# Conv taps in halves and TensorE's side work spread over the sixteen steps of a block

## The chip, the cores and the metric

The kernel runs on one core of a Trainium2 chip. The metric is the device time of one execution in microseconds (us). One execution is also recorded by the hardware profiler; durations and waits come from that one.

## The reference

Input x has shape (8, 128, 128, 128), fp32, in the order batch, channel, row, column. Two layers follow each other, and all arithmetic stays in fp32.

```python
# layer 0: dilated conv to 64 channels, batch norm, gelu, 2-D FFT, channel attention and a gate, inverse FFTs, + x
x = layer0(x)
# layer 1
y   = conv3x3(x, conv_w) + conv_b                    # 128 -> 128 channels
seq = y.reshape(B * H * W, 8, 16)                    # 8 tokens of 16 channels from each row of 128 numbers
out = mamba(seq)                                     # d_inner 32, d_state 16, 8 sequential steps:
      # h = dA * h + dBx ;  y_t = sum over d_state of h * C ;  then gate by silu(z), project back to 16
xp  = silu(group_norm(out.reshape(B, C, H, W), 4 groups) * gn_w + gn_b)
return x + xp
```

The reshape is a plain one: an image row of one channel, 128 columns long, is one sequence of 8 tokens. The state of a sequence has 32 x 16 numbers.

## The kernel before

Layer 0 handles two images at a time: a convolution phase, an attention phase and a spectrum phase. It ends at about 2.95 ms in the trace; the change leaves it alone.

Layer 1 (`layer1`) cuts the eight images into 256 blocks of RB = 4 rows, each 128 channels x 512 positions. After the transposition in `turn` the 128 partitions hold what belongs to one sequence, and N = 512 sequences lie along the free dimension. The 8 tokens are the time steps t of the recurrence; each is worked in two halves, so a block has NS = 16 steps s, with t = s // 2. The order on each engine is written out by hand: `step(i, s)` issues, for block i and its neighbours, what belongs to step s, and under the manual schedule every engine keeps that order.

What step s of block i issues, in this order:

- At s = 0, `lay_out(i, 1)` (SP's queue): 8 DMAs that spread dt and u over partitions (`du`, 64 KB each) and 8 that copy B and C to all places (`bb`, `cc`, 256 KB each, read from the tile `bc1`). Then `load(i + 2)`: at every second block a load of ten rows of the layer's input (`xin`, 640 KB).
- `spreads` of the next step: TensorE makes `da` (L543, only if t > 0) and `ups` (L544), two matmuls each on 16 rows of the array. An fp32 matmul appears as two passes in the profile. ScalarE turns `da` into an exponential (L546).
- At s = 15 `project_x(i + 2)`, at s = 0 `project_dt(i + 1)`, at s = 1 and 2 `project_bc(i + 1, 0)` and `(i + 1, 1)`, whose results ScalarE copies from PSUM to the tiles `bc0` and `bc1` (L515).
- `project_out(i - 1)` (L602) in the steps of the table OUT, `conv(i + 2)` (L134) in those of the table CONV (nine taps, each a matmul of up to 512 columns), and `turn(i + 2)` (L476) at one step. The `halves` behind the three projections of the item before are L484, `project_bc` is L513.
- `advance`: VectorE multiplies `da` by the state of the step two before and adds `h` (L567, L568). In the steps of ON_POOL the addition goes to GpSimd, and VectorE does one operation instead of two (L564, then L565 on GpSimd).
- `inject` of the next step: VectorE makes the new `h` from `ups` and `bb` (L553). `inject` j is the one that starts the state of step j.
- At s = 1 `inputs(i + 1)` on VectorE; `weigh` on GpSimd (h times `cc`, L574); at s = 15 `project_z(i + 2)`.
- Four steps behind, `collect` (TensorE, L583, every second step) sums over d_state, and at two places, s = 3 and s = 11, `skip` (TensorE, L589) and `gated` (VectorE, L594, tile `ym`) end half a block's sum.
- At s = 8 `lay_out(i + 1, 0)` and the loads of the last stage; at s = 3 the last addition on GpSimd and the store of a result block. `keep` (bn_stats on VectorE, then a store of the block for the group norm) and, at an image's end, `norm_of`.

The tiles that matter: PSUM holds `ups` once, `da` twice, `yps` once and `pm` once. Everything that isn't `ups`, `da` or `yps` uses `pm` by turns, through `misc()`:

```python
p_m = ctx.enter_context(tc.tile_pool(name="l1_pm", bufs=1, space=PSUM))
def misc():
    return p_m.tile([P, RB, W], F32, name="pm")
```

`bc0`, `bc1`, `y` and `yT` have one buffer each (pool wk1), `du`, `bb` and `cc` two, the states `h` five and the products `hc` six.

Of the kernel before, what the change touches and what calls it, by code (L numbers as in the profile page):

```python
# [9 lines left out]
F32 = mybir.dt.float32  # L10
# [6 lines left out]
P = 128  # L17
C = 128
H = 128
# [97 lines left out]
def _taps(dil):  # L117

    t = [(ky, kx) for ky in range(3) for kx in range(3)]
    t.remove((1, 1))  # L120
    return [(ky * 3 + kx, (ky - 1) * dil, (kx - 1) * dil) for ky, kx in [(1, 1)] + t]


def _conv_taps(nc, outs, wt, srcs, base, r, dil, k0=0, k1=9):

    taps = _taps(dil)
    for n in range(k0, k1):
        t, dy, dx = taps[n]  # L130
        a, b = max(0, -(r + dy)), min(4, H - (r + dy))
        wa, wb = max(0, -dx), min(W, W - dx)
        for out, src in zip(outs, srcs):
            nc.tensor.matmul(  # L134
                out[:, a:b, wa:wb], wt[:, t, :],
                src[:, r + dy + a - base:r + dy + b - base, wa + dx:wb + dx],
                start=(n == 0), stop=(n == len(taps) - 1),
            )


# [203 lines left out]
def layer1(ctx, tc, x1, w1, c1, out):  # L344
# [8 lines left out]
    nc = tc.nc  # L353
# [5 lines left out]
    wt = const.tile([P, W1_N], F32, name="l1_wt")  # L359
# [3 lines left out]
    def cf(name):  # L363
        at, n = C1[name]
        return ct[:, at:at + n]

    def wf(name):
        at, n = W1[name]
        return wt[:, at:at + n]

    convw = wf("conv_w").rearrange("p (t c) -> p t c", c=C)
# [15 lines left out]
    taps = cf("taps").rearrange("p (k l) -> p k l", l=L)  # L387
    w_k = wf("conv1d_w").rearrange("p (k d) -> p k d", d=DI)
    with tc.tile_pool(name="l1_prep", bufs=2) as prep:
# [19 lines left out]
        for hf in range(NH):  # L409
            for l in range(L):  # L410
                k = hf * L + l
# [14 lines left out]
    RB = 4  # L426
    N = RB * C
    GP = 2
    NS = L * NG // GP
    wk1 = ctx.enter_context(tc.tile_pool(name="l1_w1", bufs=1))  # L430
    wk2 = ctx.enter_context(tc.tile_pool(name="l1_w2", bufs=2))
# [8 lines left out]
    blocks = [(b, r) for b in range(B) for r in range(0, H, RB)]  # L440
    nb = len(blocks)
    st8 = [{} for _ in blocks]
    xins, stats, gns, tails = {}, {}, {}, []
    ON_POOL = (5, 8, 11, 14)

    def live(i):
        return 0 <= i < nb

    def misc():
        return p_m.tile([P, RB, W], F32, name="pm")  # L450

    def load(i):
        b, r = blocks[i]
        if r % CH == 0:
            lo, hi = max(0, r - 1), min(H, r + CH + 1)
            xin = wk2.tile([P, CH + 2, W], F32, name="xin")
            nc.sync.dma_start(xin[:, :hi - lo, :], x1[b][:, lo:hi, :])
            xins[b, r // CH] = xin, lo
        st8[i]["xin"] = xins[b, r // CH]

    def conv(i, k0, k1):
        d = st8[i]
        if k0 == 0:
            d["pm"] = misc()
        xin, lo = d["xin"]
        _conv_taps(nc, [d["pm"]], convw, [xin], lo, blocks[i][1], 1, k0, k1)
        if k1 == 9:
            y = wk1.tile([P, RB, W], F32, name="y")
            nc.scalar.activation(y, d["pm"], AF.Identity, bias=wf("conv_b"))
            d["y"] = y  # L470
# [16 lines left out]
    def project_x(i):  # L487
        d = st8[i]
        ps = halves([m_xh[:, hf, :] for hf in range(NH)], [d["yT"]] * NH)
        d["xc"] = wk3.tile([P, NH, N], F32, name="xc")  # L490
        nc.scalar.activation(d["xc"], ps, AF.Silu, bias=wf("conv1d_b"))
# [13 lines left out]
    def inputs(i):  # L505
        d = st8[i]
        d["u"] = wk2.tile([P, NH, N], F32, name="u")
        nc.vector.tensor_mul(d["u"], d["dt"], d["xc"])
# [8 lines left out]
    def lay_out(i, hf):  # L517

        d = st8[i]
        du = wk2.tile([P, LP, N], F32, name="du")  # L520
        bb = wk2.tile([P, LP, N], F32, name="bb")
        cc = wk2.tile([P, LP, N], F32, name="cc")
        for q in range(NG):
            for k, v, g in ((0, d["dt"], q), (8, d["u"], (q + GP) % NG)):
                nc.sync.dma_start(du[q * DI + k:q * DI + k + 8], v[g * DI:(g + 1) * DI, hf, :])
        for lp in range(LP):
            for k, v in ((0, bb), (1, cc)):
                at = (k * LP + lp) * DS
                nc.sync.dma_start(
                    v[:, lp, :], d["bc", hf][at:at + DS, :].unsqueeze(1).broadcast_to([DS, 8, N]))  # L530
        d["du", hf], d["bb", hf], d["cc", hf] = du, bb, cc
# [24 lines left out]
    def advance(i, s):  # L556
# [3 lines left out]
        if t:  # L560
            da, before = d["da", s], d["h", s - 2]
            if s in ON_POOL:
                ah = wk1.tile([P, GP, N], F32, name="ah")
# [26 lines left out]

    def gated(i, hf):
        d = st8[i]
        d["ym", hf] = wk1.tile([P, N], F32, name=f"ym{hf}")
        nc.vector.tensor_mul(d["ym", hf], d["yps"], d["zs"][:, hf, :])  # L594

    def project_out(i, k0, k1):
# [12 lines left out]
    def keep(i):  # L609
        d, (b, r) = st8[i], blocks[i]  # L610
        if r == 0:
            gns[b] = dram.tile([C, H, W], F32, name="gn")
            stats[b] = wk2.tile([P, H // RB, nc.vector.BN_STATS_DIM], F32, name="st")
        nc.vector.bn_stats(stats[b][:, r // RB, :], d["xr"].rearrange("p a b -> p (a b)"))
        nc.sync.dma_start(gns[b][:, r:r + RB, :], d["xr"])
        d.clear()

    def norm_of(b):

        mv = wk2.tile([P, 2], F32, name="mv")  # L620
        gmv = wk2.tile([P, 2], F32, name="gmv")
        dv = wk2.tile([P, 1], F32, name="dv")
        sc = wk2.tile([P, 1], F32, name="sc")
        bi = wk2.tile([P, 1], F32, name="bi")
        nc.vector.bn_aggr(mv, stats[b])
        ps = misc().rearrange("p a b -> p (a b)")
        nc.tensor.matmul(ps[:, 0:2], cf("group"), mv, start=True, stop=True)
        nc.vector.tensor_copy(gmv, ps[:, 0:2])
        nc.vector.tensor_sub(dv, mv[:, 0:1], gmv[:, 0:1])
        nc.vector.tensor_mul(dv, dv, dv)  # L630
        ps = misc().rearrange("p a b -> p (a b)")
        nc.tensor.matmul(ps[:, 0:1], cf("group"), dv, start=True, stop=True)
        nc.vector.tensor_scalar(sc, ps[:, 0:1], gmv[:, 1:2], GN_EPS, ALU.add, ALU.add)
        nc.scalar.activation(sc, sc, AF.Sqrt)
        nc.vector.reciprocal(sc, sc)
        nc.vector.tensor_mul(sc, sc, wf("gn_w"))
        nc.vector.tensor_mul(bi, gmv[:, 0:1], sc)
        nc.vector.tensor_sub(bi, wf("gn_b"), bi)
        tails.extend((b, r, sc, bi) for r in range(0, H, RB))
# [11 lines left out]
    def last_act():  # L651
        b, r, sc, bi, v, res = fin["active"] = fin.pop("loaded")
        nc.scalar.activation(v, v, AF.Silu, bias=bi, scale=sc)  # L653
# [3 lines left out]
        nc.gpsimd.tensor_add(res, res, v)  # L657
        nc.sync.dma_start(out[b, :, r:r + RB, :], res)  # L658

    CONV = {7: (0, 2), 8: (2, 3), 9: (3, 5), 10: (5, 6), 11: (6, 7), 12: (7, 8), 13: (8, 9)}  # L660
    OUT = {5: (0, 5), 6: (5, 8)}

    def step(i, s):

        ni, ns = (i, s + 1) if s + 1 < NS else (i + 1, 0)
        if s == 0:
            if live(i):
                lay_out(i, 1)  # L670
            if live(i + 2):
                load(i + 2)
        if live(ni):
            spreads(ni, ns)
        if s == 15 and live(i + 2):
            project_x(i + 2)
        if s == 0 and "loaded" in fin:
            last_act()
        if s == 0 and live(i + 1):
            project_dt(i + 1)  # L680
        if s in (1, 2) and live(i + 1):
            project_bc(i + 1, s - 1)
        if s in OUT and live(i - 1):
            project_out(i - 1, *OUT[s])
        if s in CONV and live(i + 2):
            conv(i + 2, *CONV[s])
        if s == 14 and live(i + 2):
            turn(i + 2)
        if live(i):
            advance(i, s)  # L690
        if live(ni):
            inject(ni, ns)
        if s == 1 and live(i + 1):
            inputs(i + 1)
        if live(i):
            weigh(i, s)
        if s == 15 and live(i + 2):
            project_z(i + 2)

        gi, gs = (i, s - 4) if s >= 4 else (i - 1, s - 4 + NS)  # L700
        if live(gi):
            if gs % 2 == 0:
                collect(gi, gs // 2)
            if gs in (7, 15):
                skip(gi, gs // 8)
                gated(gi, gs // 8)
        if s == 8:
            if live(i + 1):
                lay_out(i + 1, 0)
            if tails:  # L710
                last_load()
        if s == 3 and "active" in fin:
            last_sum()
        if s == 7 and live(i - 1):
            keep(i - 1)
        if s == 3 and live(i - 2) and blocks[i - 2][1] + RB == H:
            norm_of(blocks[i - 2][0])

    E = mybir.EngineType
    with tc.manual_schedule(engines={E.PE, E.Activation, E.DVE, E.Pool, E.SP}):  # L720
# [92 lines left out]
```

## Time and profile before

| | |
|---|---|
| median of 3 runs | 19169.76 us (19157.88 to 19195.24) |
| the profiled execution, its own time | 19192.02 us |
| its span in the profile | 19190.2 us |
| mean granted TensorE clock | 0.862 |
| TensorE matmul busy | 18443.3 us (96%) |
| VectorE busy | 13878.4 us (72%) |
| GpSimd busy | 12632.6 us (66%) |
| ScalarE busy | 7032.3 us (37%) |
| DMA engines, mean busy share | 45.9% on SP's queue |

A matmul's end is modelled in the profile, and TensorE counts as busy while a matmul runs at half clock, so the 96% is no measure of how much of the array is used. The granted clock is listed for any stretch of time. Of a group of instructions the profile gives the busy time and mean duration, then the idle time of its engine just before them and the instruction that ended most of it. In a list of stretches each line has the stretch, its length, the busy time of TensorE (matmuls), TensorE's weight loads, VectorE, ScalarE and GpSimd with their counts of instructions, then the granted clock, the DMA engines' busy share and GB/s. In a timeline a line has the start, the duration, the engine (SPq: a DMA issue on SP's queue), the line of the kernel and the operation; brackets tell how long the engine was idle before it.

### The profile page before, as it was taken

What the parts mean: (1) busy time and instruction counts of PE and PEld (TensorE: products, weight loads), DVE (VectorE), ACT (ScalarE), POOL (GpSimd) and SP (SyncE); (2) the same over time, 40 slices, a digit from 0 to 9 for tenths busy, and PEclk for the clock granted to TensorE, in tenths of its full rate; (3) what the DMA queues carried; (4) which work ended last, traced back from release to release, by engine and by line L of the source; (5) the groups of instructions that cost most, each with busy time, mean ns of one, the idle gap of its engine ahead of it and who ended that gap; (6) DMA issues with size and microseconds to landing.
All of it is one profiled execution on the core that took longest, in us unless ns stands there. A gap on an engine that the chain in (4) does not pass through costs nothing. (4 is left out here: it accounts for less than half of the span.)

```text
span 19190.2 us, 208781 instructions
## 1 busy us (share of the span) xinstructions
PE 18443.3 (96%) x74920; PEld 6645.5 (35%) x74920; DVE 13878.4 (72%) x14203; ACT 7032.3 (37%) x7703; POOL 12632.6 (66%) x5636
## 2 busy tenths in 40 slices
PE   8998999999999999999999999999999999999997
PEld 3554553333333333333333333333333333333332
DVE  1441447778778877787788877887787878877885
ACT  1131223333333433333334333433333333333333
POOL 0010015777777777777777777777777777777776
PEclk9999998888888888888888888888888888888886
DMA  2222224444455555555555545555555555555555
GB/s 85 70 76 83 75 73 91 93 96 94 97 106 106 107 105 106 108 104 104 108 106 106 109 102 107 108 108 104 106 107 106 106 105 108 105 104 109 106 106 122
DMA packets 1075786, 1932.99 MB, mean 101 GB/s; under 512 B 123968, under 2 KB 255040, under 8 KB 1058368
## 3 DMA queue, kind: packets, MB, share of 16 engines
q1 hardware_dynamic: 1001472, 1850.17, 45.9%
q10 hardware_dynamic: 73280, 69.47, 1.3%
q8 instruction: 596, 9.76, 0.2%
q14 instruction: 438, 3.59, 0.1%
HBM read 375.64 MB, written 201.33 MB: 30 GB/s over the span
## 5 line engine op out<-in xcount | busy, mean ns | idle before, releaser
L574 POOL TENSOR_TENSOR hc<-h,cc 128x1024 f32<-128x1024 f32 x4096 | 9604.0, 2356 | 3447.5 <-PE pm L513 1304.7
L553 DVE TENSOR_TENSOR h<-ups,bb 128x1024 f32<-128x1024 f32 x4096 | 4993.9, 1219 | 2903.9 <-PE ups L544 2546.7
L543 PE MATMUL da<-du,m_a 16*128 16x512 f32 x14336 | 6343.9, 728 | 210.0 <-DVE h L568 193.2
L546 ACT ACTIVATE da<-da 128x1024 f32<-128x1024 f32 x3584 | 3617.9, 1010 | 7110.2 <-PE ups L544 7106.1
L544 PE MATMUL ups<-du,m_u 16*128 16x512 f32 x16384 | 5410.2, 737 | 9.7 <-DVE h L553 2.6
L568 DVE TENSOR_TENSOR h<-da,h 128x1024 f32<-128x1024 f32 x2560 | 3134.0, 1224 | 87.8
L567 DVE TENSOR_TENSOR da<-da,h 128x1024 f32<-128x1024 f32 x2560 | 3132.2, 1224 | 65.0 <-ACT da L546 62.8
L543 PEld LDWEIGHTS da<-du,m_a 16*128 16x128 f32 x14336 | 1789.2, 206 | 3402.2 <-DVE h L568 1717.1
L583 PE MATMUL yps<-hc,l_ct 128*32 128x512 f32 x16384 | 2824.9, 769 | 1.7 <-POOL hc L574 1.7
L565 POOL TENSOR_TENSOR h<-ah,h 128x1024 f32<-128x1024 f32 x1024 | 2420.7, 2364 | 392.0 <-DVE ah L564 391.8
L134 PE MATMUL pm<-xin,l_wt 128*128 128x508 f32 (+1 forms) x4608 | 2447.4, 632 | 5.2 <-DMA l_wt<-w 4.6
L544 PEld LDWEIGHTS ups<-du,m_u 16*128 16x128 f32 x16384 | 1410.6, 207 | 1661.3 <-DVE h L553 1015.8
L134 PEld LDWEIGHTS pm<-xin,l_wt 128*128 128x128 f32 x4608 | 732.8, 189 | 1616.3 <-issue 1613.0
L272 POOL TENSOR_TENSOR xr<-xr,sq 128x512 f32<-128x512 f32 x128 | 160.5, 1266 | 1652.6 <-ACT sq L271 1603.5
L564 DVE TENSOR_TENSOR ah<-da,h 128x1024 f32<-128x1024 f32 x1024 | 1240.9, 1212 | 0.0
L602 PEld LDWEIGHTS pm<-m_o,ym 128*128 128x128 f32 x4096 | 909.7, 327 | 767.1 <-issue 766.3
L134 PE MATMUL cps<-xin,l_wt 128*64 128x500 f32 (+2 forms) x4608 | 1026.7, 584 | 39.1 <-issue 30.2
L602 PE MATMUL pm<-m_o,ym 128*128 128x128 f32 x4096 | 1060.1, 440 | 0.6 <-DVE ym L594 0.6
L222 DVE COPY fT<-tps 128x512 f32<-128x512 f32 x128 | 88.5, 692 | 1182.2 <-PE tps L221 1182.2
L583 PEld LDWEIGHTS yps<-hc,l_ct 128*32 128x32 f32 x16384 | 355.4, 119 | 1354.9 <-issue 1282.3
L338 POOL TENSOR_TENSOR og<-og,xg 128x512 f32<-128x512 f32 x128 | 164.4, 1285 | 967.1 <-ACT og L337 831.6
L515 ACT COPY bc<-pm 128x512 f32<-128x512 f32 x512 | 301.6, 589 | 1041.0 <-DMA cc<-bc 594.9
(145 smaller groups left out, 13471.5 us busy)
## 6 DMA issues: line engine op xcount, KB each, us to landing
bb<-bc SPq DMA_DIRECT2D x2048, 256.0 KB
cc<-bc SPq DMA_DIRECT2D x2048, 256.0 KB
du<-dt SPq DMA_DIRECT2D x2048, 64.0 KB
du<-u SPq DMA_DIRECT2D x2048, 64.0 KB
xin<-x SPq DMA_DIRECT2D x112, 640.0 KB
xin<-x SPq DMA_DIRECT2D x48, 1408.0 KB
gn<-xr SPq DMA_DIRECT2D x256, 256.0 KB
v<-gn SPq DMA_DIRECT2D x256, 256.0 KB
```

The lines of the kernel that those rows point to most:

```text
L134: nc.tensor.matmul(out[:, a:b, wa:wb], wt[:, t, :], src[:, r + dy + a - base:r + dy + b - base, wa + dx:wb + dx], start=(n == 0), stop=(n ...
L543: nc.tensor.matmul(da[:, q], m_a[a:a + 16, :], du[a:a + 16, lp, :], start=True, stop=True)
L544: nc.tensor.matmul(ups[:, q], m_u[u:u + 16, :], du[u:u + 16, lp, :], start=True, stop=True)
L546: nc.scalar.activation(da, da, AF.Exp)
L553: nc.vector.tensor_mul(h, d["ups", s], bb[:, lp:lp + 1, :].broadcast_to([P, GP, N]))
L564: nc.vector.tensor_mul(ah, da, before)
L565: nc.gpsimd.tensor_add(h, ah, h)
L567: nc.vector.tensor_mul(da, da, before)
L568: nc.vector.tensor_add(h, da, h)
L574: nc.gpsimd.tensor_mul(hc, d["h", s], cc[:, lp:lp + 1, :].broadcast_to([P, GP, N]))
L583: nc.tensor.matmul(d["yps"][g * DI:(g + 1) * DI], gather[:, lp, :], d["hc", 2 * t + g // GP][:, g % GP], start=(lp == 0), stop=False, skip ...
L602: nc.tensor.matmul(d["pm"][:, j, :], d["ym", hf][:, j * C:(j + 1) * C], m_of[:, hf, :], start=(hf == 0), stop=(hf == NH - 1))
```

## The change

- A tap of layer 1's convolution becomes two matmuls of two rows (up to 256 columns) each; the eighteen halves are issued in steps 3 to 10 instead of nine whole taps in steps 7 to 13.
- `turn` moves from step 14 to step 11, `project_out` from steps 5 and 6 to steps 12 and 13. For that, `ym` gets two buffers.
- The steps in which GpSimd does the addition become 3, 7, 11 and 14 instead of 5, 8, 11 and 14.
- `keep` moves from step 7 of the next block to step 0 of the one after it, `norm_of` from step 3 to the same step 0.

Lines from L129 on stand two lines lower in the kernel after.

```diff
-def _conv_taps(nc, outs, wt, srcs, base, r, dil, k0=0, k1=9):
+def _conv_taps(nc, outs, wt, srcs, base, r, dil, k0=0, k1=9, parts=1):
     taps = _taps(dil)
-    for n in range(k0, k1):
+    for k in range(k0, k1):
+        n, rows = k // parts, 4 // parts
         t, dy, dx = taps[n]
         a, b = max(0, -(r + dy)), min(4, H - (r + dy))
+        a, b = max(a, k % parts * rows), min(b, (k % parts + 1) * rows)
         wa, wb = max(0, -dx), min(W, W - dx)
         for out, src in zip(outs, srcs):
             nc.tensor.matmul(
                 out[:, a:b, wa:wb], wt[:, t, :],
                 src[:, r + dy + a - base:r + dy + b - base, wa + dx:wb + dx],
-                start=(n == 0), stop=(n == len(taps) - 1),
+                start=(k == 0), stop=(k == parts * len(taps) - 1), skip_group_check=(parts > 1),
             )
...
-    ON_POOL = (5, 8, 11, 14)
+    ON_POOL = (3, 7, 11, 14)
...
-        _conv_taps(nc, [d["pm"]], convw, [xin], lo, blocks[i][1], 1, k0, k1)
-        if k1 == 9:
+        _conv_taps(nc, [d["pm"]], convw, [xin], lo, blocks[i][1], 1, k0, k1, 2)
+        if k1 == 18:
...
-        d["ym", hf] = wk1.tile([P, N], F32, name=f"ym{hf}")
+        d["ym", hf] = wk2.tile([P, N], F32, name=f"ym{hf}")
...
-    CONV = {7: (0, 2), 8: (2, 3), 9: (3, 5), 10: (5, 6), 11: (6, 7), 12: (7, 8), 13: (8, 9)}
-    OUT = {5: (0, 5), 6: (5, 8)}
+    CONV = {3: (0, 1), 4: (1, 3), 5: (3, 6), 6: (6, 8), 7: (8, 11), 8: (11, 13), 9: (13, 16), 10: (16, 18)}
+    OUT = {12: (0, 2), 13: (2, 8)}
...
-        if s == 14 and live(i + 2):
+        if s == 11 and live(i + 2):
             turn(i + 2)
...
-        if s == 7 and live(i - 1):
-            keep(i - 1)
-        if s == 3 and live(i - 2) and blocks[i - 2][1] + RB == H:
-            norm_of(blocks[i - 2][0])
+        if s == 0 and live(i - 2):
+            b, r = blocks[i - 2]
+            keep(i - 2)
+            if r + RB == H:
+                norm_of(b)
```

## The prediction

> **What bounds the kernel now.** I read the sums first (the costliest groups), then the waits, then one block of the second layer in the timeline, then the same block cut into stretches of 3.413 us.
>
> ```profile
> L574 POOL TENSOR_TENSOR hc<-h,cc 128x1024 f32<-128x1024 f32 x4096 | 9604.0, 2356 | 3447.5 <-PE pm L513 1304.7
> L553 DVE TENSOR_TENSOR h<-ups,bb 128x1024 f32<-128x1024 f32 x4096 | 4993.9, 1219 | 2903.9 <-PE ups L544 2546.7
> L134 PE MATMUL pm<-xin,l_wt 128*128 128x508 f32 (+1 forms) x4608 | 2447.4, 632 | 5.2 <-DMA l_wt<-w 4.6
> ```
>
> The 4096 `inject` multiplications (L553) mark the steps (`inject` j is issued in step j - 1). The first starts at 2979.9, that of the last block's first step at 18985.5: 255 periods of 62.77 us. That is 83% of the span, and all that the diff touches. Back to back, a VectorE operation of 1024 elements starts every 1.18 us. A block has 41 of these (16 `inject`, 20 at L567/L568, 4 at L564, 1 at L508), two gated products and one bn_stats: 50.2 us. GpSimd needs 20 x 2.36 + 1.28 = 48.5 us. So neither sum is the bound; VectorE waits 10 us a block for TensorE (2546.7 / 256). The stretches show why:
>
> ```profile
> 10097.26:10100.67 3.41, 3.41 (x18) 0.99 (x18) 3.38 (x4) 0.00 (x0) 2.35 (x1) 1.00 0.86 159
> 10100.67:10104.09 3.42, 3.20 (x14) 0.79 (x17) 3.42 (x4) 1.52 (x3) 2.23 (x1) 1.00 0.05 13
> 10104.09:10107.50 3.41, 3.30 (x13) 0.94 (x12) 3.38 (x4) 0.99 (x1) 2.73 (x3) 0.50 0.20 77
> 10107.50:10110.91 3.41, 3.41 (x15) 1.91 (x12) 2.27 (x3) 1.01 (x1) 3.33 (x3) 0.50 0.00 0
> 10110.91:10114.33 3.42, 3.42 (x15) 1.69 (x14) 2.53 (x3) 0.66 (x1) 3.42 (x2) 0.50 0.00 0
> 10114.33:10117.74 3.41, 3.41 (x17) 1.29 (x19) 3.04 (x3) 0.93 (x2) 1.41 (x2) 0.50 0.23 88
> 10117.74:10121.15 3.41, 3.41 (x20) 0.99 (x12) 2.52 (x3) 1.01 (x1) 2.15 (x1) 1.00 0.35 85
> ```
>
> The column after POOL is the granted clock. It drops to half for four stretches where the convolution is absent (steps 4 to 7), and once more around steps 14 and 15: about 17 us of 61.4. TensorE counts as busy throughout, so busy time doesn't decide. I counted work instead: each 512-column pass as 0.43 us, times the share of the 128x128 array it uses (0.125 for a `spreads` pass, 0.25 for `collect`, 1 for the rest; shorter passes by their columns). In all 508 drops after 3072 us the stretch before holds at most 0.375 of its length in full-array work; of 2712 stretches that kept full clock, 95% hold over 0.42. The return comes after a half-clock stretch with at least 0.358 in the same units. So one stretch under about 1.28 us of full-array work costs the clock.
>
> **What the skill says.** The Trainium skill, "TensorE: Matmul & The Clock Gate", Part 1: a free-running 3413 ns window, and half or full clock set by recent activity. The trace agrees on both (boundaries on that grid, 0.50 or 1.00). The page speaks of idle windows; here the drop follows a window with 3.20 us of 3.42 busy, and the measurement decides. The same page, Part 3, has matmuls strictly in issue order: one that waits blocks all behind it. "PSUM — Partial Sum Buffer", Specifications: 8 banks of 512 fp32 values per partition. The pools use 2 + 4 + 1 + 1, hence one single `pm` tile for `project_bc`, `conv`, `turn` and `project_out`.
>
> **The change without a new wait.** Times from one `inject` to the next, from this block at full clock: 3.53 where VectorE alone counts (three operations); 2.49 where the sum is on GpSimd (`inject`, 1.04 of spreads, two handovers); 3.99 and 4.68 from steps 1 and 2.
> - `turn` leaves step 14, where at half clock it and `collect` held back step 15 (0 starts 4.11 after 15, 1 another 4.70 later). After, step 0's spreads start when `inject` 15 is done (1.2, and 0.1 for the handover); from their start to `inject` 1 it is 6.03 in this block (10083.41 to 10089.44, the spreads of steps 0 and 1 and `project_x`, `project_z` between, at full clock): 7.33 for both.
> - ON_POOL (3, 7, 11, 14): steps 3 and 7 become 2.49; 5 and 8 become 3.53. GpSimd has as many sums as before.
> - `gated` (0.65) waits for `skip`. Step 4: 4.45. Step 12: 4.86 less the tap (about 0.95) plus `turn` (about 0.5), so 4.5.
> - bn_stats (0.65 in step 8) moves behind step 1's `inject`, where VectorE idles 2.76: nothing.
> - Half taps: 18 matmuls for 9, same columns, 9 more weight loads. No 256-column tap is in the trace; L288 has 256 columns, and its passes start 0.22 to 0.32 apart, so 0.44 to 0.64 a half tap against 0.86 to 1.06 a whole one: 0 to 1.9 us a block. I take 0.1 a step with taps; steps 4 to 10 then need at most 3.0 of TensorE against 3.53. Hidden; without that cover, up to 1.9.
> - `ym` with two buffers takes away a wait that isn't in the waits: nothing. The gn store moves to step 0 on SP's queue, behind `lay_out` and `load`; SP's wait for `xr` (11 us a block) goes, and SP next waits for the spreads of step 6, as now.
> Sum: 7.33 + 3.99 + 4.68 + 4.45 + 4.5 + 3 x 2.49 (3, 7, 11) + 2.49 (14) + 6 x 3.53 (5, 6, 8, 9, 10, 13) = 56.1 us. By this, 6.7 a block would be won.
>
> **The wait that the change adds.** `conv` now begins in step 3, on the `pm` tile that `project_bc(1)` filled in step 2. ScalarE may copy that out only when the previous `bc1` has been read by the 8 DMAs of `lay_out(i, 1)`, and these are issued only after the block's last spread:
>
> ```profile
> 10080.63 0.74 SPq L525 DMA_DIRECT2D du<-dt  x1
> 10096.12 1.53 SPq L529 DMA_DIRECT2D cc<-bc  x1
> 10096.22 1.12 PE L513 MATMUL pm<-xc,m_bc 128*128 128x512 f32 x2 [0.38 <-ACT bc L515]
> 10101.88 0.59 ACT L515 COPY bc<-pm 128x512 f32<-128x512 f32 x1 [4.79 <-PE yps L589]
> ```
> ```profile
> ACT bc L515 <- DMA cc<-bc: 594.9, 153, 6.4
> ```
>
> The spread ends at 10080.56; the copy starts 21.3 us after `inject` 15, 20.8 to 22.2 in nine blocks of ten. Today nobody needs `pm` before step 5, and it costs nothing. After, step 3's half tap is due at 18.35 (counted from `inject` 15) and gets `pm` at 21.95. Behind it in TensorE's order stand `skip` and the spreads of step 5; `gated` waits for `skip`, and on VectorE step 4's advance waits for `gated`.
>
> Every second block also loads `xin`, behind these DMAs:
>
> ```profile
> 10142.10 0.74 SPq L525 DMA_DIRECT2D du<-dt  x1
> 10159.69 1.19 SPq L457 DMA_DIRECT2D xin<-x  x1
> ```
>
> The last packet of that load ends at 10165.4 in the trace; I take 23.4 with the handover. Today's step 7 is far behind it; step 3 is not.
>
> TensorE then stands still for over 3 us, so a stretch under 1.28 is certain and tap and `skip` run at half clock (0.9 + 1.85). `inject` 5 comes at 21.95 + 2.75 + 0.05 + 0.65 + 2.35 = 27.75 instead of 22.94: +4.8. With the load +6.2. Where the return takes one stretch more, spreads of step 6 are late: 0.4 and 0.1 on average. Mean: 56.1 + (5.2 + 6.3) / 2 = 61.9.
>
> A second gap remains around step 13: from `collect` of step 12 to `project_out` a stretch may hold only 0.94. It does if it starts within a 1.7 us range, half of all phases. The drop costs 0.6 when six projections lift the clock at once, 3.5 when it lasts into `project_x`: 0.85 on average, 0.25 more for nearby borderline stretches. **62.77 becomes about 63.05**, 0.28 x 255 = +71 us: 19192 (this execution: span 19190.2 and 2 around it) becomes 19263. It lies 22 above the median of the runs, so 19240 against 19170.
>
> **Rivals.**
> A, faster: the clock isn't lost, because a short true pause may count otherwise than the thin work seen today, and step 13 falls well. Then tap and `skip` take 1.45: 59.6 and 61.05, mean 60.3: 19192 - 2.47 x 255 - 22 = 18540. Against: no drop without a thin stretch, no long thin stretch without a drop. It decides as soon as `conv`'s late start and both drops together cost under 6.7 us.
> B, much faster: `pm` comes free in time, 56.1: 17,470. For it only that I read the dependence from one wait; against, 255 blocks with the copy at 21.
> C, slower: after the pause the half clock lasts. Saturated at half clock, two steps take 10.1 us and hold 3.87 of work, 0.38: on the threshold. If it or step 13's drop costs one stretch more in each block, 63.05 + 2.35 = 65.4: 19,840. For it: a further half stretch at steps 15 and 0 costs 2.1 us today (from `inject` 0 to 1: median 4.70, the longest tenth over 6.81). Against: `conv` and `collect` together make 3.6 us of dense work in even steps, which lifts the clock within three stretches.
> D, the half taps do not do what they say: 1.9 us a block exposed, +480. It needs TensorE full in steps 4 to 10; it isn't at full clock.
>
> **Numbers.** About 0.2% is what a measurement of this kernel can tell from no change. Likeliest case 0.48 (period 62 to 64, alone 18,960 to 19,480: 0.12 faster, 0.08 same, 0.28 slower); A 0.28; B 0.04; C with D 0.20. Faster 0.44, same 0.08, slower 0.48. Range 18,540 to 19,750: it leaves out B and the far ends of A and C.
>
> **What would show it.** Right: a new wait of TensorE's L136 for ScalarE's `bc` copy (L517), once a block, 3 to 5 us, with the copy still 21 us after `inject` 15; VectorE waiting for `skip` before L596 for about 4 us; half clock in steps 3 to 5 and now and then 13 to 15, none left in 5 to 7; steps 7 to 11 at 2.49 and 3.53. Wrong: L136 without that wait; full clock through step 3; or half clock through steps 4 to 10.

## The result, and the profile after

| | before | after |
|---|---|---|
| median of 4 runs each | 19163.82 us (19148.3 to 19195.24) | 19314.74 us (19287.36 to 19320.31) |
| the profiled execution, its own time | 19192.02 us | 19320.31 us |
| mean granted TensorE clock | 0.862 | 0.909 |
| period of a block (mean, `inject` to `inject`) | 62.77 us | 63.25 us |

The change makes the kernel slower by 0.7%: ratio 1.0074, 95% interval 1.0056 to 1.0091. A run more than 1.5% above the fastest of its kernel stays out of every ratio; among all runs that is one of the twelve of e4. TensorE runs at a higher clock than before, and the time grew all the same. The period explains it: 255 x (63.25 - 62.77) = 122 of the 128 us between the two profiled executions.

The costliest groups, from the page of the kernel after (busy time, mean of one | idle time before it, and what ended most of that):

```profile
L555 DVE TENSOR_TENSOR h<-ups,bb 128x1024 f32<-128x1024 f32 x4096 | 4989.7, 1218 | 1661.5 <-PE ups L546 890.4
L576 POOL TENSOR_TENSOR hc<-h,cc 128x1024 f32<-128x1024 f32 x4096 | 9595.4, 2356 | 3989.1 <-issue 1457.2
L136 PE MATMUL pm<-xin,l_wt 128*128 128x254 f32 (+2 forms) x9216 | 2785.0, 433 | 1199.4 <-DMA xin<-x 681.0
L596 DVE TENSOR_TENSOR ym<-yps,zs 128x512 f32<-128x512 f32 x512 | 354.1, 692 | 1616.2 <-PE yps L591 1586.3
```

The wait of `inject` for `ups`, which carried the kernel before (2546.7 us), fell to 890.4: the evening-out works. Two other waits took its place. The convolution's matmuls (L136) now idle for 1199.4 us where they idled for 5.2, and `gated` (L596) waits 1586.3 us for `skip`, where in the kernel before it waited for 167.2 (us in total, times, longest):

```profile
DVE ym L594 <- PE yps L589: 167.2, 258, 4.8
```

The waits of the kernel after say who keeps them:

```profile
DVE ym L596 <- PE yps L591: 1586.3, 260, 8.7
...
ACT bc L517 <- DMA cc<-bc: 779.8, 117, 15.7
PE pm L136 <- DMA xin<-x: 681.0, 123, 13.9
...
PE pm L136 <- ACT bc L517: 505.4, 125, 6.0
ACT bc L517 <- DMA gn<-xr: 498.8, 74, 8.6
```

The chain reads from below: ScalarE's copy of `bc1` (L517) waits for DMAs, the first half tap (L136) waits for that copy in one block (125 times, 4.0 us each) and for the `xin` load in the next (123 times, 5.5 us each), and VectorE's `gated` waits for `skip`, which stands behind the half tap in TensorE's order. One block in the timeline of the kernel after (start, duration; in brackets the idle time of the engine before it):

```profile
10015.22 1.23 DVE L555 TENSOR_TENSOR h<-ups,bb 128x1024 f32<-128x1024 f32 x1 [0.20 <-issue]
...
10018.50 0.59 ACT L517 COPY bc<-pm 128x512 f32<-128x512 f32 x1 [6.85 <-DMA bb<-bc]
...
10019.14 1.22 PE L136 MATMUL pm<-xin,l_wt 128*128 128x256 f32 x2 [4.07 <-ACT bc L517]
...
10020.16 1.91 PE L591 MATMUL yps<-xc,m_d 128*128 128x512 f32 x2
...
10022.11 0.69 DVE L596 TENSOR_TENSOR ym<-yps,zs 128x512 f32<-128x512 f32 x1 [5.67 <-PE yps L591]
...
10025.12 1.21 DVE L555 TENSOR_TENSOR h<-ups,bb 128x1024 f32<-128x1024 f32 x1
```

From one `inject` to the next it is 9.9 us in place of 4.5: VectorE stands still for 5.67 us, and half tap and `skip` take 2.9 us since the clock is at half. The same place in stretches of 3.413 us (TensorE's matmuls, weight loads, VectorE, ScalarE, GpSimd, then the clock, the DMA share and GB/s):

```profile
10013.20:10016.62 3.42, 1.88 (x8) 0.31 (x6) 3.05 (x3) 0.00 (x0) 3.42 (x2) 1.00 0.93 167
10016.62:10020.03 3.41, 0.89 (x2) 0.80 (x3) 0.00 (x0) 1.50 (x2) 3.33 (x3) 0.50 0.29 83
10020.03:10023.45 3.42, 3.42 (x11) 0.90 (x10) 1.34 (x2) 0.00 (x0) 1.16 (x1) 0.50 0.20 77
10023.45:10026.86 3.41, 3.41 (x12) 1.38 (x12) 3.38 (x4) 1.01 (x1) 1.53 (x1) 0.50 0.00 0
10026.86:10030.27 3.41, 3.41 (x26) 1.68 (x22) 3.38 (x4) 1.01 (x1) 1.94 (x2) 1.00 0.02 5
```

The pause begins in the first stretch and fills most of the second; the clock drops behind the first and stays down for three. All 399 drops between the first `inject` and that of the last block follow a stretch with at most 0.375 of full-array work, counted as in the prediction. Half clock takes 12.5 us a block where it took 19.5.

### The profile page after: what moved, and what is told of

Same layout as the page of the kernel before. It is cut to its first block, busy times and chain, and to the rows that moved or that the text cites. A ratio compares the mean times of both kernels' runs of the same rounds, so it can differ in the third digit from the quotient of the medians.

```text
span 19318.5 us, 217481 instructions
## 1 busy us (share of the span) xinstructions
PE 17393.9 (90%) x79528; PEld 7314.5 (38%) x79528; DVE 13847.9 (72%) x14203; ACT 6999.2 (36%) x7696; POOL 12606.1 (65%) x5636
## 5 line engine op out<-in xcount | busy, mean ns | idle before, releaser
L555 DVE TENSOR_TENSOR h<-ups,bb 128x1024 f32<-128x1024 f32 x4096 | 4989.7, 1218 | 1661.5 <-PE ups L546 890.4
L545 PE MATMUL da<-du,m_a 16*128 16x512 f32 x14336 | 5902.2, 680 | 122.9 <-DVE h L570 121.8
L546 PE MATMUL ups<-du,m_u 16*128 16x512 f32 x16384 | 5002.5, 676 | 97.7 <-DVE h L555 94.5
L136 PE MATMUL pm<-xin,l_wt 128*128 128x254 f32 (+2 forms) x9216 | 2785.0, 433 | 1199.4 <-DMA xin<-x 681.0
L569 DVE TENSOR_TENSOR da<-da,h 128x1024 f32<-128x1024 f32 x2560 | 3131.1, 1223 | 17.6 <-ACT da L548 17.6
L136 PEld LDWEIGHTS pm<-xin,l_wt 128*128 128x128 f32 x9216 | 1708.4, 205 | 3036.2 <-issue 1663.4
L567 POOL TENSOR_TENSOR h<-ah,h 128x1024 f32<-128x1024 f32 x1024 | 2416.2, 2360 | 0.9 <-DVE ah L566 0.9
L585 PE MATMUL yps<-hc,l_ct 128*32 128x512 f32 x16384 | 2323.6, 641 | 3.4 <-POOL hc L576 3.4
L596 DVE TENSOR_TENSOR ym<-yps,zs 128x512 f32<-128x512 f32 x512 | 354.1, 692 | 1616.2 <-PE yps L591 1586.3
L136 PE MATMUL cps<-xin,l_wt 128*64 128x500 f32 (+2 forms) x4608 | 1025.7, 584 | 38.5 <-issue 30.1
L517 ACT COPY bc<-pm 128x512 f32<-128x512 f32 x512 | 301.6, 589 | 1697.9 <-DMA cc<-bc 779.8
L604 PEld LDWEIGHTS pm<-m_o,ym 128*128 128x128 f32 x4096 | 643.9, 240 | 400.4 <-issue 399.7
L604 PE MATMUL pm<-m_o,ym 128*128 128x128 f32 x4096 | 754.3, 342 | 0.6 <-DVE ym L596 0.6
```

Of the source, the lines that this page charges most:

```text
L136: nc.tensor.matmul(out[:, a:b, wa:wb], wt[:, t, :], src[:, r + dy + a - base:r + dy + b - base, wa + dx:wb + dx], start=(k == 0), stop=(k ...
L545: nc.tensor.matmul(da[:, q], m_a[a:a + 16, :], du[a:a + 16, lp, :], start=True, stop=True)
L546: nc.tensor.matmul(ups[:, q], m_u[u:u + 16, :], du[u:u + 16, lp, :], start=True, stop=True)
L555: nc.vector.tensor_mul(h, d["ups", s], bb[:, lp:lp + 1, :].broadcast_to([P, GP, N]))
L567: nc.gpsimd.tensor_add(h, ah, h)
L569: nc.vector.tensor_mul(da, da, before)
```

## The experiments

Theory: the loss is the wait on the shared `pm` tile and on `xin`, plus the drop of the clock that the wait sets off. Rivals: the clock (not the wait) carries it; the order on TensorE carries it; the half taps carry it. Each ratio is to runs of the kernel before on the same chip; periods and steps come from the profiles. "Step j" below means the time from `inject` j to `inject` j + 1. Times and clocks of steps are means from block 20 on, and a period is the mean of all blocks. Line numbers are those of each kernel.

### e1_bc_two: two buffers for `bc0` and `bc1`

```diff
-        d["bc", hf] = wk1.tile([P, N], F32, name=f"bc{hf}")
+        d["bc", hf] = wk2.tile([P, N], F32, name=f"bc{hf}")
```

> The kernel after, with two buffers for each of bc0 and bc1, so that ScalarE's copy no longer waits for the DMAs of lay_out. If the late pm tile is the cause: blocks without a load of xin get the tap at about 18.4 us after inject 15 instead of 22.7 and take about 56.8 us instead of 62.4; blocks with a load still wait for xin until 23.9 and stay at 64.0. Mean period 60.4 instead of 63.25: about 18590. Rival (the half taps or GpSimd's new steps eat the gain, the wait is only where the slack shows): no change, 19315.

Measured: 18603.56 us, ratio 0.9702 (0.9688 to 0.9717), period 60.51. Blocks without a load take 57.13 us, with `inject` 5 at 23.35 after `inject` 15 (28.59 in the kernel after); blocks with a load take 63.82, their first tap at 24.00 (23.94). So the wait for `bc1` is real and worth about 5.3 us in the blocks where it ends last; in the others the load ends last, and nothing is gained.

### e2_load_early: the load of `xin` eight steps earlier

```diff
         if s == 0:
             if live(i):
                 lay_out(i, 1)
-            if live(i + 2):
-                load(i + 2)
...
             if tails:
                 last_load()
+            if live(i + 3):
+                load(i + 3)
```

> The kernel after, with the load of xin issued in step 8 of the block before instead of behind lay_out in step 0. If xin costs what the difference of the two kinds of blocks says (64.0 against 62.4 us), all blocks take about 62.4: about 19100. Rival (blocks with a load are longer because their 640 KB crowd the other DMAs, wherever they are issued): 19250 to 19315.

Measured: 19071.43 us, ratio 0.9947 (0.9932 to 0.9962), period 62.29. Step 4 falls from 10.47 to 9.60 us only: with the load out of the way the copy of `bc1` is still late in every block.

### e3_both: both edits together

The diffs of e1 and e2 in one kernel.

> The kernel after with both: two buffers for bc0 and bc1, and xin loaded in step 8. If the two waits and the half clock that they cause are all that the change lost: the sum of the steps without a wait, 56.1 us, and about 0.9 for the clock's drop around step 13: 57 us a block, about 17720. TensorE's L136 then waits for neither ScalarE's bc copy nor xin, and the clock is full in steps 3 to 10. Rival (another engine takes over as the bound, GpSimd's 48.5 us or SP's queue): 58.5 to 61, 18100 to 18750.

Measured: 17912.85 us, ratio 0.9338 (0.9323 to 0.9354), period 57.85. What TensorE's convolution idles for, in the answer for line L136 of this kernel (us, times):

```profile
  issue: 2212.2, 4203
  DMA l_wt<-w: 19.3, 3
  DMA xin<-x: 5.2, 5
  ACT bc L517: 2.2, 2
```

`issue` is idle time in which nothing that the profile shows was waited for; most of it stands before weight loads, and layer 0's convolution is counted in. In the kernel after the same answer has 1122.9 us for `bc` and 686.2 for `xin`. Both waits are gone, and with them 5.4 us a block. The clock is 1.0 in steps 3 to 10. The forecast was 17720: steps 14, 15 and 0 take 2.88 + 3.67 + 4.65 us, at clocks of 0.80, 0.83 and 0.92. The thin place around step 13 was still costing.

### e4_fill: full-array work in the pause, the waits left

Four matmuls of 512 columns in step 3, ahead of the half tap, into the `da` tile of the next spreads.

```diff
-        da = p_a.tile([P, GP, N], F32, name="da") if t else None
+        da = d.pop("early", None)
+        if t and da is None:
+            da = p_a.tile([P, GP, N], F32, name="da")
...
+    def fill(i):
+        ps = st8[i]["early"] = p_a.tile([P, GP, N], F32, name="da")
+        for k in range(4):
+            nc.tensor.matmul(ps[:, k % GP], m_dtf, st8[i]["xc"][:, k % NH, :], start=True, stop=True)
...
+        if s == 3 and live(i) and live(i + 2):
+            fill(i)
```

> The kernel after, with four more matmuls of 512 columns on the whole array in step 3 ahead of the first half tap, into the da tile that step 4 overwrites: results unused. They fill 3.8 us of TensorE's wait for pm. If half of the loss there is the clock: it stays full through the tap and skip, which take 1.45 us instead of 2.9; period about 61.7 instead of 63.25, about 18930: more work, less time. Rival (the clock doesn't follow the array's work, or only the wait counts): 19315, or up to 19450 where the four come too late.

Measured: 19204.28 us (12 runs, 19030.40 to 19320.57), ratio 1.0003 (0.9978 to 1.0028), period 62.91. The filling does its part in its own place: step 4 falls from 10.47 to 8.83 us, its clock rises from 0.617 to 0.993. But steps 14, 15 and 0 grow from 10.33 to 11.71 (2.95 + 3.67 + 5.09, clocks 0.756, 0.829, 0.872) and give nearly all of it back. The forecast of 18930 missed because it took the gain of one place for the gain of the block.

### e5_conv_last: half taps behind `skip` and `gated` within a step

```diff
-        if s in CONV and live(i + 2):
-            conv(i + 2, *CONV[s])
...
             if gs in (7, 15):
                 skip(gi, gs // 8)
                 gated(gi, gs // 8)
+        if s in CONV and live(i + 2):
+            conv(i + 2, *CONV[s])
```

> The kernel after, with conv issued last among TensorE's work of its step, behind collect, skip and gated; nothing else. The half tap of step 3 gets pm as late as before (22.7 and 23.9 us after inject 15), but skip no longer stands behind it. If the order on TensorE is how the wait reaches VectorE, gated comes at about 20 and inject 5 waits only for the tap and the spreads behind it: 2.8 us a block earlier, about 18600. Rival (what counts is the idle clock and TensorE's sum, not who stands behind the tap): 19200 to 19315.

Measured: 19028.48 us, ratio 0.9929 (0.9907 to 0.9951), period 62.14. `gated` starts at 20.10 us after `inject` 15 in a block without a load and 19.78 with one (25.59 and 26.88 in the kernel after), as meant. `inject` 5 comes only 2.5 us earlier. The late copy of `bc1` has a second way to VectorE, over ScalarE: there the exponential of step 4 stands behind the copy, and VectorE's `advance` of step 4 (L569) now waits for it 243 times, 720.9 us in total, where in the kernel after, with `gated` late, it waited twice, 17.1 us. The pause of TensorE is still there too, and behind it the taps that were held back run at half clock and delay step 5 (4.83 us, clock 0.635), 6 (3.67) and 7 (2.91). The forecast of 18600 missed. The order on TensorE is a part of the loss, not its source.

### e7_half_taps_only: the kernel before with half taps in its own steps

```diff
-    CONV = {7: (0, 2), 8: (2, 3), 9: (3, 5), 10: (5, 6), 11: (6, 7), 12: (7, 8), 13: (8, 9)}
+    CONV = {7: (0, 4), 8: (4, 6), 9: (6, 10), 10: (10, 12), 11: (12, 14), 12: (14, 16), 13: (16, 18)}
```

with `_conv_taps` and `conv` as in the change.

> The kernel before, with only the taps in halves, in the same steps as its whole taps. If the nine additional matmuls and weight loads are hidden beside VectorE, 0 to 0.4 us a block: 19170 to 19270. Rival (they are exposed as the prediction's D says, 1.9 us a block): about 19650.

Measured: 19192.72 us (12 runs), ratio 1.0013 (1.0003 to 1.0023), period 62.73. The group on the page of this kernel:

```profile
L136 PE MATMUL pm<-xin,l_wt 128*128 128x254 f32 (+2 forms) x9216 | 2457.3, 399 | 5.1 <-DMA l_wt<-w 4.5
```

Twice as many passes, 399 ns where a whole tap's took 632, and nearly the same busy time (2447.4 before). Half taps cost 0.03 to 0.23% here by the ratio's interval, at most 0.2 us a block; rival D had 1.9.

### e6_before_both: both edits of e3 on the kernel before

> The kernel before with the same two edits as e3 (two buffers for bc0 and bc1, xin loaded in step 8). Its conv starts in step 7 and its pm tile isn't wanted before step 5, so both waits are hidden: no change, 19130 to 19200. Rival (bc's wait on ScalarE costs the kernel before too, through the exponential that stands behind it): 0.3 to 1 us a block faster, 18920 to 19100.

Measured: 18916.99 us, ratio 0.9864 (0.9844 to 0.9884), period 61.71. "No change" missed: with the two waits the kernel before is 1.0 us a block slower. The 0.25 us of step 4 (4.50 to 4.25) are the late copy, as the rival has it: VectorE's L567 waited 62.8 us for the exponential behind the copy, 87 of the 90 times in step 4, and waits 0.4 us in e6. The rest lies in steps where the clock changes: step 0 (5.35 to 4.81, clock there 0.906 to 0.985), 14 and 15 (0.4 less together) and 7 (0.2 more). The median of step 0 stays at 4.70, and 192 of the 255 blocks of e6 take 61.44 us, 18 stretches of 3.413, within 0.05 (34 in the kernel before); how the waits cost this rest isn't shown, nor which of the two edits gains it. In the kernel after the same edits gain 5.4.

### e8_both_out4: e3 with `project_out` shared evenly

```diff
-    OUT = {12: (0, 2), 13: (2, 8)}
+    OUT = {12: (0, 4), 13: (4, 8)}
```

> As e3 (both waits taken away), with project_out dealt out as 4 and 4 matmuls over steps 12 and 13 instead of 2 and 6. Counted as in the prediction, every stretch between steps 12 and 14 then holds 1.26 to 1.29 us of full-array work, on the threshold, where e3 had down to 0.94. If the count holds, the drop around step 13 becomes rarer: 0.3 to 1.4 us a block, 17550 to 17830 against e3's 17913. Rival (the drops at steps 13 to 0 have another cause): 17913.

Measured: 18422.24 us, ratio 0.9613 (0.9595 to 0.9631), period 59.75: 1.9 us a block worse than e3. Stretches around step 13 of one block:

```profile
10074.33:10077.75 3.42, 3.23 (x19) 1.46 (x19) 3.38 (x4) 1.59 (x2) 2.43 (x2) 1.00 0.02 7
10077.75:10081.16 3.41, 3.41 (x14) 0.63 (x14) 2.35 (x3) 1.36 (x2) 3.41 (x2) 0.50 0.00 0
10081.16:10084.57 3.41, 3.41 (x9) 1.00 (x6) 3.07 (x3) 0.93 (x1) 3.33 (x3) 0.50 0.38 91
```

TensorE is busy for 3.23 of 3.42 us ahead of the drop, yet by the count of the prediction this stretch holds 0.36 of full-array work. The edit puts that count at 0.36 to 0.37 in nearly every block, so the clock falls in nearly every one, and the half clock lasts into step 0 (6.60 us, clock 0.725). The even share is worse here than the uneven one because it lands just under the threshold.

### e10_both_again: e3 with 1.7 us more of full-array work

`project_out`'s first pair is issued three times more behind `collect` in step 12, its last pair once more in step 13; the copy out of `pm` follows the last.

```diff
         if s in OUT and live(i - 1):
             project_out(i - 1, *OUT[s])
+            if s == 13:
+                project_out(i - 1, 6, 8, True)
+                copy_out(i - 1)
...
+            if s == 12 and live(i - 1):
+                for _ in range(3):
+                    project_out(i - 1, 0, 2, True)
```

> As e3, but some of project_out's matmuls are issued again, with the same result: in step 12, after collect, the first pair three times more, and in step 13 the last pair once more. That is 1.7 us more of full-array work in each block, put where TensorE would stand idle. If the thin stretch is the cause, the clock stays full in steps 13 to 0 (e3: 0.96, 0.80, 0.83, 0.92), and steps 14, 15 and 0 take 9.8 us instead of 11.2: about 17560, less time for more work. Rival (TensorE's load itself is the limit there): 17913 to 18350.

Measured: 17570.12 us (17566.9 to 17576.34), ratio 0.9169 (0.9152 to 0.9186), period 56.44 (median block 56.15). The kernel does more and takes 343 us less than e3. The granted clock over the span, in the pages of the kernel after and of this one (40 slices):

```profile
PEclk9999999889999989999898898988998888889987
```
```profile
PEclk9999999999999999999999999999999999999997
```

The median block is what the prediction's sum without a new wait gave, 56.1.

### e9_fill_again: the kernel after with the fillings of e4 and e10, its waits left

> The kernel after with both fillings and both waits left in: e4's four matmuls ahead of the first half tap and e10's repeated matmuls of project_out. The clock should stay full in the whole block, so that only the waits remain: e4's step 4 (8.8 us instead of 4.4) on e10's 56.4, that is 60.7 to 60.9 us a block, 18650 to 18720; from 19315, this is what the clock cost of the change's loss, and from 17570 what the waits cost. Rival (the clock drops elsewhere instead): 19000 to 19200.

Measured: 18859.85 us, ratio 0.9834 (0.9817 to 0.9851), period 61.43; step 4 takes 9.40 us at a clock of 0.979, all other steps run at about 1. Of the 6.8 us between the kernel after (63.25) and e10 (56.44), the waits are 61.43 - 56.44 = 5.0 and the clock 63.25 - 61.43 = 1.8; in the other order, e3 and then e10, they are 5.4 and 1.4. The forecast of 18650 to 18720 gave the wait 0.5 to 0.8 us too little. With its waits left and its clock kept the changed kernel is 1.7% faster than the kernel before; without, it is 0.7% slower. One wait less turns the sign as well: e1 is 3.0% and e2 0.5% faster than the kernel before.

### e11_again_pool_old: e10 with GpSimd's sums where they were

```diff
-    ON_POOL = (3, 7, 11, 14)
+    ON_POOL = (5, 8, 11, 14)
```

> As e10, with GpSimd's sums back in steps 5, 8, 11 and 14. VectorE's operations are as many, and by the sum of the steps 3 and 7 get longer by what 5 and 8 get shorter: no change, 17500 to 17650. Rival (the new steps for GpSimd's sums are part of the gain, since 5 and 8 stand three steps apart from the next and GpSimd falls behind): 0.5 to 1.5 us a block, 17700 to 17950.

Measured: 17426.21 us (17419.05 to 17429.15), ratio 0.9087 (0.9071 to 0.9102), period 55.86: the best version, 9% under the kernel before. "No change" missed, and the rival has the wrong sign: steps 3 to 8 take 19.79 us instead of 20.34 together. With the sum in step 3, VectorE comes to `gated` early and waits there for `skip` (step 4 takes 4.40 us against 4.14), and step 7 takes 2.73 us where a step with the sum on GpSimd takes 2.55 (step 5 of this kernel): `inject` waits there for GpSimd (26.0 us, 70 times, between 8000 and 12000 us of e10; 0.5 us, once, in this kernel).

### e13_before_filled: e6 with filling where its clock falls

One matmul of 512 columns more at the end of steps 3 and 4, into the `pm` tile that `project_out` then overwrites. (e12_before_filled, with a `pm` tile of its own for them, which nobody reads, has no time: the engines wait for each other without end.)

```diff
+        if s in (3, 4) and live(i - 1) and live(i):
+            d = st8[i - 1]
+            if s == 3:
+                d["pm"], d["early"] = misc(), True
+            nc.tensor.matmul(
+                d["pm"].rearrange("p a b -> p (a b)"), m_dtf, st8[i]["xc"][:, 0, :], start=True, stop=True)
```

> As e6 (the kernel before with two buffers for bc0 and bc1 and xin loaded in step 8), with one more matmul of 512 columns on the whole array at the end of steps 3 and 4, into the pm tile that project_out overwrites in step 5: 1.7 us more of full-array work a block. The order of everything else is that of before. If the four half-clock stretches of steps 4 to 7 come from the thin stretches of steps 3 to 5, they go: 4, 5, 6 and 7 take 4.13 + 2.5 + 3.53 + 3.53 instead of 17.1 us, so 58.3 us a block, about 18060; the drop at steps 14 and 15 stays. Rival (the change's new order is needed for the clock): 18900 or slower.

Measured: 18900.99 us, ratio 0.9869 (0.9852 to 0.9886), period 61.63: the same as e6, where 18060 was expected. Steps 4 to 7 fall from 17.06 to 13.95 us at full clock, and steps 14, 15 and 0 rise from 11.60 to 14.71. Stretches of one block, from step 13 on:

```profile
10053.06:10056.48 3.42, 3.20 (x10) 0.81 (x10) 3.38 (x4) 1.70 (x2) 2.23 (x2) 1.00 0.13 50
10056.48:10059.89 3.41, 3.40 (x15) 1.43 (x18) 2.32 (x3) 1.22 (x2) 3.41 (x2) 0.50 0.00 0
10059.89:10063.30 3.41, 3.41 (x12) 0.51 (x4) 2.37 (x3) 1.65 (x2) 3.33 (x3) 0.50 0.35 87
10063.30:10066.72 3.42, 3.42 (x6) 1.52 (x5) 1.23 (x1) 0.00 (x0) 3.35 (x2) 0.50 0.69 81
10066.72:10070.13 3.41, 3.41 (x10) 1.17 (x9) 0.17 (x1) 2.45 (x3) 0.57 (x1) 1.00 0.97 150
```

The drop before this one came at 9995.04, the next at 10117.92: 61.44 us apart, 18 windows of 3.413, as are 246 of this kernel's 262 distances between drops. One thin place was filled, and the block came to rest with the other one in a window of its own. The 3.1 us won were lost again to a tenth. A filling of both places of the kernel before wasn't tried, so what its own schedule is worth at full clock stays open.

## Why the prediction was right, and where it was off

It said 19240 against 19170, with a period of 63.05; the period is 63.25, the time 19315. Its own terms, 56.1, 5.75 for the wait and 1.1 for the drop around step 13, add up to 62.95, not to 63.05.

- **The wait that the change adds**: right in place, size and kind. TensorE's L136 waits 4.0 us for ScalarE's copy in blocks without a load (3 to 5 said), the load takes over in the others, and e3 takes both away. The copy comes 22.0 us after `inject` 15 in blocks without a load (21.3 said), the first tap at 22.66 (21.95) and 23.94 (23.4), tap and `skip` take 2.89 (2.75), and `inject` 5 comes at 28.59 and 29.88 (27.75 and 29.15). VectorE's wait for `skip` is 6.1 us (1586.3 over 260) where about 4 was said. The copy is late by 0.7 probably because the store for the group norm now follows the DMAs of `lay_out` at once in SP's queue; the waits name `gn` 74 times as what ended it. The prediction priced that move at nothing. This is argued, not isolated.
- **The clock falls with a true pause**: right. Step 4 has a clock of 0.617 and e4 and e9 take it to 0.98 or 0.99. Rival A is out. "None left in 5 to 7" was too hopeful: step 5 has 0.797 and takes 3.82 instead of 3.53, so steps 4 and 5 together are 0.56 over the sum's.
- **The sum without a new wait**: 56.1 said, 56.15 in the median block of e10. Single terms: steps 15 and 0 together 7.31 in the medians (7.33), step 1 4.05 (3.99), step 2 4.68, step 12 4.37 (4.5), steps 3, 7 and 11 2.58, 2.69 and 2.58 (2.49), the rest 3.53 or 3.54.
- **The drop around step 13**: the place was right, its size not. It was put at 1.1 us a block and measures 0.54 over steps 14, 15 and 0. This error and the 0.56 of steps 4 and 5 cancel, which is luck: each is twice the 0.28 us by which the period was to grow. What remains is 0.38 for steps 3, 7 and 11, and small terms.
- **GpSimd's sums at no cost**: wrong. "As many sums as before" counted instructions, not what waits beside them. e11 puts the move at 0.55 us a block.
- **"Today nobody needs `pm` before step 5, and it costs nothing"**: wrong. e6 shows that late copy and late load together cost the kernel before 1.0 us a block. A quarter of it is the copy, over the exponential behind it on ScalarE, a way that the prediction left out; the rest stays open.
- **Half taps hidden**: right, by e7 and by steps 5, 6, 8, 9 and 10 of e3, which take 3.53 or 3.54 us; rival D is out. Rival C's mechanism, half clock that lasts while held-back work is caught up, appears in e5, not as its 2.35 us a block in the kernel after.

The change's own aim is therefore sound: with both waits taken away from either kernel, the new order takes 57.85 us (e3) and the old one 61.71 (e6), and filled it takes 56.44 (e10). What a filled kernel in the old order would take isn't known. The loss came of the waits together with the drop of the clock behind them, and taking away either wait, that for `bc1` or that for `xin`, would have been enough for a gain.

## What to carry to other kernels

Before work is moved to an earlier step, look up who held its buffers at that step: a wait that costs little in the old place can, in the new one, stop an engine that works in order, and everything behind it. Follow the late buffer on every engine that touches it: taken out of one engine's order (e5), the wait came back over another's. Where the clock depends on how much of the array is used in a fixed window, judge a move by the thinnest window of the whole loop: filling one thin place let the next one take the loss (e4, e13), and an even share just under the threshold was worse than an uneven one (e8). Moving a sum to another engine is not free because the count is the same: check what the relieved engine meets next.

## What the runs showed of the hardware

- The clock follows array work rather than busy time: it fell after 3.20 us (e13) and 3.23 us (e8) of 3.42 busy. In the traces of all fourteen kernels, after 3072 us, 3811 stretches at full clock were followed by a drop and 49658 were not. One limit, 0.376 on the count of the prediction, has 248 of them on the wrong side; a limit on TensorE's busy share, chosen for each trace as the best one, has 1965. The Trainium skill, "TensorE: Matmul & The Clock Gate", Part 1, has the window free-running at 3413 ns, which the trace shows; its split into busy and idle windows doesn't tell these from kept ones.
- More matmuls can take less time: 1.7 us of full-array work added to each block of e3 took 1.4 us off its period.
- A loop can fall into step with the window: e13's drops lie 18 windows apart, 192 blocks of e6 and 195 of e13 take these 61.44 us within 0.05, and a saving of 3.1 us in one part of the block left its period where it was (61.63 against 61.71 us).
